# Moving the last output tiles of an attention kernel to the end of their periods, and summing them in another buffer

## The chip, the cores and the metric

The kernel runs on one core of a Trainium2 chip. A core has five engines with queues of their own: TensorE (PE) for matrix products, VectorE (DVE), ScalarE (ACT), GpSimd (POOL), and SyncE (SP), which in this kernel issues every DMA. Each engine works through its queue strictly in the order in which the program wrote it, and waits where an operand isn't ready. PE writes into PSUM, a memory of its own; the other data lie in SBUF. The metric is the device time in microseconds (us).

## The reference, cut to what matters

Two layers work on x of shape (2, 2048, 512): two batches of 2048 rows with 512 features. The first is a state space layer with a feed-forward part and is not touched by the change. The second is self-attention with 16 heads of 32 features, whose norm is modulated by a condition:

```python
h = _sln(hidden, w, ...)                       # layer norm, times gamma, plus beta
qkv = (h @ Wqkv.T + bqkv).reshape(B, N, num_heads, hd, 3)
energy = jnp.einsum('bhqd,bhkd->bhqk', q, k)
att = jax.nn.softmax(energy, axis=-1) / D ** 0.5
out = jnp.einsum('bhqk,bhkd->bhqd', att, v)
out = out @ Wp.T + bp
h1 = out + hidden
h2 = _sln(h1, w, ...)
return h2 + h1
```

The change concerns the last four lines: the projection, the sum with `hidden`, and the second norm with the sum `h2 + h1`. With the row mean m and the reciprocal deviation s, one row of the output is (h1 - m) * s * gamma + beta + h1. The constants of the norm are folded into two rows that are the same for all rows of a batch, `g_row` and `t_row`.

## The kernel before, in words

The attention runs in blocks. A block is one batch, one pair of heads and one chunk of 512 queries; there are 2 x 8 x 4 = 64 blocks. A block has 16 tiles of keys (128 keys each) and takes eight periods of two key tiles. The order of all work is written by hand: one loop over periods `j` (from -22 to 513) issues the instructions, and since every engine works in order, the place in this loop is the place in each engine's queue.

In one period, the loop issues, in this order:

- what is due at its start (a list filled by `after(j, ...)`),
- `make`: scores of one key tile on PE, from which DVE takes off the maximum (L805),
- `compare`: scores that DVE only uses for a running maximum of a later block (L771),
- `exponentials` of the first key tile on ACT (L810),
- `keep`: scores of a later block, copied to SBUF by ACT (L762) and put into the running maximum by DVE (L767),
- `exponentials` of the second key tile,
- what is due at its end (a list filled by `closing(j, ...)`),
- `take_off`: POOL takes the maximum off kept scores that the next period uses (L799, 2.39 us each, 704 of them),
- `weighted`: PE multiplies the probabilities of the period before with the values (L820).

Scores are kept and compared 14 periods ahead. So from period 498 on, PE has no scores to make ahead. PSUM has three slots called `s` for scores; the projections of output tiles take one of them too. Kept scores lie in a ring of 22 buffers, `ring`.

When a block is done, its result and its row sums go to DRAM. When all head pairs of a chunk are done, the chunk's output tiles of 128 rows can be finished. Each batch has 16 such tiles, `qt` 0 to 15. Those of the first batch (b = 0) are finished while the second batch's attention runs. Those of the second batch (b = `LB` = 1) come at the very end. The last two head pairs of the second batch are ordered so that chunks 0, 1 and 2 are done by periods 480, 488 and 496. Their tiles, `qt` 0 to 11, run beside the remaining attention, one every two periods; the change concerns these twelve. The last chunk's four tiles (`qt` 12 to 15) are done together after the last block by `end_last`.

A tile `qt` of the second batch passes through these functions. The first column is the period relative to its start k, where k = 484 + 2 qt:

| period | function | what it issues |
|---|---|---|
| k | `fetch` | SP: loads `o4` (the attention's result), `by` (reciprocal row sums, four DMAs) and `xr` (x plus the bias) |
| k + 2 | `divide` | POOL: `o4` times `by` (L878) |
| k + 3 | `project` | PE: four products into `py` in PSUM (L891) |
| k + 3 | `residual` | DVE: `xr` = `py` + `xr` (L898), which is h1 |
| k + 3 | `statistics` | DVE: mean and variance, first guess of the reciprocal root |
| k + 4 | `deviation` | DVE: three turns of Newton's method on one column, and `shift` |
| k + 5 | `last_norm` | ACT: `z` = normed h1, into PSUM (L958); DVE: `y` = `z` times `g_row` (L960) |
| k + 6 | `last_close` | POOL: h1 + `t_row` (L965), then `y` plus that (L966); SP: stores `y` (L967) |

All of these are issued with `after`, at the start of the period. `y` has one buffer; `xr` has three.

The tiles of the first batch take another way through `turns` (Newton on POOL), `gain` (DVE: `w` = (h1 - m) * `g_row`, and `xr` = h1 + `t_row`, L933 and L934), `scaled` (ACT: `w` times s, L939) and `close` (POOL: one sum, L944; SP: store). Their projections and DVE work are issued with `closing`, at the end of a period. h1 stays in PSUM there.

Near the end, `end_sums`, `end_weights`, `end_sums_more` and `end_x` load what the last chunk needs, also through SP. `end_begin` and `end_project` do part of its projection on PE in periods 510 and 511.

Of the kernel before, what the change touches and what calls it, by code (L numbers as in the profile page):

```python
# [14 lines left out]
ALU = mybir.AluOpType  # L15
# [4 lines left out]
P = 128  # L20
# [19 lines left out]
def tile_s5_block_then_sln_attention(  # L40
# [21 lines left out]
    nc = tc.nc  # L62
# [3 lines left out]
    TT = CH // P  # L66
# [5 lines left out]
    NQ = L // CH  # L72
# [29 lines left out]
    x2 = [dpool.tile([L, D], F32, name=f"x2_{b}") for b in range(NB)]  # L102
# [457 lines left out]
    spare = ps1.tile([P, TT, D], F32, name="spare", tag="po", bufs=1)  # L560
# [47 lines left out]
    for name, src in (("wk", w_kT), ("wq", w_qT), ("wv", w_vT)):  # L608
        w = wlate.tile([P, KC, D], F32, name=name)
# [229 lines left out]
    held, ending = {}, {}  # L839
# [21 lines left out]
    def fetch(b, qt):  # L861

        at = slice(qt * P, (qt + 1) * P)
        o4 = work.tile([P, NG, P], F32, name="o4")
        nc.sync.dma_start(o4, od[b][:, at].rearrange("(g r) q -> r g q", r=P))
        by = work.tile([P, NG, P], F32, name="by")
        heads = invd[b][:, at].rearrange("(g j) q -> j g q", j=4)
        for j in range(4):
            nc.sync.dma_start(
                by[32 * j : 32 * j + 32, :, :], heads[j : j + 1, :, :].to_broadcast([32, NG, P])  # L870
            )
        xr = work.tile([P, D], F32, name="xr", bufs=3)
        nc.sync.dma_start(xr, x2[b][at, :])
        held[b, qt] = o4, by, xr

    def divide(b, qt):
        o4, by, xr = held[b, qt]
# [16 lines left out]
    def residual(b, qt):  # L894

        o4, xr, py = held[b, qt]
        if b == LB:
            nc.vector.tensor_add(xr, py, xr)  # L898
            held[b, qt] = xr, xr, None
        else:  # L900
            nc.vector.tensor_add(py, py, xr)
            held[b, qt] = py, xr, o4.rearrange("p g q -> p (g q)")

    def statistics(b, qt):

# [14 lines left out]
    def newton(eng, y, v):  # L920

        for _ in range(3):
            c = small.tile([P, 1], F32, name="c3")
            eng.tensor_scalar(c, y, y, v, ALU.mult, ALU.mult)
            eng.tensor_scalar(y, c, 1.5, y, ALU.add, ALU.mult)

    def turns(b, qt):
        newton(nc.gpsimd, *held[b, qt][-2:])

    def gain(b, qt):  # L930

# [31 lines left out]
    def last_close(b, qt):  # L963
        h, y = held.pop((b, qt))
        nc.gpsimd.tensor_tensor(h, h, ending[b][1], ALU.add)  # L965
        nc.gpsimd.tensor_tensor(y, y, h, ALU.add)  # L966
        nc.sync.dma_start(out[b, qt * P : (qt + 1) * P, :], y)  # L967

    LB, LC = NB - 1, NQ - 1

    def spare(name):
        return ring.tile([P, 2, CH], F32, name=name, tag="x")
# [121 lines left out]
    for i in range(NP):  # L1097
        w = 2 if i in twice else 1
# [16 lines left out]
    def after(j, what, *args):  # L1115

        due.setdefault(j, []).append((what, args))

    def closing(j, what, *args):

        due.setdefault(j + 0.5, []).append((what, args))
# [13 lines left out]
    for b in range(NB):  # L1135
        for c in range(NQ):
            j = NP * (blocks.index((b, NPAIR - 1, c)) + 1) + 1
            if (b, c) == (LB, LC):
                most, rest = slice(0, NH - 4), slice(NH - 4, NH - 2)
                j = NP * (N - 1)  # L1140
                after(j - 5, fetch_sums, b, c, most)
                after(j - 3, invert, b, c, most)
                for g in range(NG - 1):
                    after(j - 2 + g, end_sums, g)
                after(j + 1, end_weights)
                after(j + 1, end_sums_more)
                after(j + 2, end_x)
                after(j + 1, fetch_sums, b, c, rest, 32)
                after(j + 4, invert, b, c, rest, 32)
                after(j + 5, end_divisors, NG - 1, 2, 1)  # L1150
                for g in range(NG - 1):
                    after(j + 3 + g, end_divide, g)
                for e in (1, 2):
                    after(j + 8, end_divide, NG - 1, slice(HD * e, HD * e + HD))
                after(j + 6, end_begin, 0)
                for g in range(NG - 1):
                    after(j + 6 + g // 2, end_project, 0, [g])
                continue
            after(j, fetch_sums, b, c)
            after(j + 2, invert, b, c)  # L1160
            if c == 0:
                after(j + 2, last_rows, b) if b == LB else after(NP * (NPAIR * NQ * (b + 1) + 2), last_rows, b)
            for t in range(TT):
                qt = c * TT + t
                if b == LB:
                    k = j + 3 + 2 * t
                    after(k, fetch, b, qt)
                    after(k + 2, divide, b, qt)
                    after(k + 3, project, b, qt)
                    after(k + 3, residual, b, qt)  # L1170
                    after(k + 3, statistics, b, qt)
                    after(k + 4, deviation, b, qt)
                    after(k + 5, last_norm, b, qt)
                    after(k + 6, last_close, b, qt)
                else:

                    k = NP * (NPAIR * NQ * (b + 1) + 2 + 3 * qt // 2)
                    after(k, fetch, b, qt)
                    after(k + 3, divide, b, qt)
                    for g in range(NG):  # L1180
                        closing(k + 5 + g // 2, project, b, qt, (g,))
                    closing(k + 7, residual, b, qt)
                    closing(k + 8, statistics, b, qt)
                    closing(k + 9, gain, b, qt)
                    after(k + 11, turns, b, qt)
                    closing(k + 12, scaled, b, qt)
                    after(k + 14, close, b, qt)
# [5 lines left out]
    def block_at(j):  # L1193
        n, i = divmod(j, NP)
        return (n, i) if 0 <= n < N else (None, i)

    for j in range(FIRST, NP * N + 2):
# [20 lines left out]
        now, k = block_at(j)  # L1218
# [89 lines left out]
```

## Time and profile before

| | |
|---|---|
| median of three runs | 3430.34 us (3430.2 to 3431.68) |
| profiled execution | 3433.31 us, its span 3431.5 us |
| mean granted TensorE clock | 0.991 |
| busy: PE, DVE, ACT, POOL | 97%, 62%, 57%, 62% of the span |
| `take_off` L799 | 704 x 2392 ns on POOL |
| projection L891 | 8 records, some 3.5 to 3.7 us a tile, from 3267.5 for tile 0 to 3387.7 for tile 11 |
| L965 and L966 on POOL | 12 each, median 1277 and 1280 ns |
| last result of the attention read from PSUM (L1043) | 3407.4 us |

The span is the time from the first to the last instruction in the profile. A stretch of the trace is named by its start and end in microseconds from the start of the span. A matrix product in 32-bit floats stands as two records in the trace. A group of instructions is named by its line in the kernel: L799 is line 799. In a table of waits, "A <- B" says that A's engine stood still until B was done. "DMA by<-invd" is the transfer that loads `by` from the DRAM tensor `invd`; "SPq" is the queue of SP.

### The profile page before, as it was taken

The page shows a single profiled execution, that of the slowest core. Times are in us where ns is not written, and L with a number is a line of the kernel's source. Part 1 is how long each engine was busy: PE and PEld are TensorE (multiplying, and loading weights), DVE is VectorE, ACT ScalarE, POOL GpSimd, SP SyncE. Part 2 cuts the span into 40 slices and gives each one's busy share as a digit, 9 for nine tenths or more (in the row PEclk, how much of TensorE's full clock was granted, in tenths as well). Part 3 has the DMA queues.
Part 4 walks back from the last instruction along what each step waited for, and adds up shares of the span by engine and source line. Part 5 has one row for each costly group of instructions (what it writes and reads, how often), then busy time and mean ns, then how long its engine had stood idle before and what let it go on. Part 6 is the DMA issues. An engine that isn't in the chain of part 4 may idle for free.

```text
span 3431.5 us, 33641 instructions
## 1 busy us (share of the span) xinstructions
PE 3333.8 (97%) x11380; PEld 1450.9 (42%) x11380; DVE 2129.4 (62%) x2720; ACT 1950.2 (57%) x2208; POOL 2140.0 (62%) x1162
## 2 busy tenths in 40 slices
PE   7999999999999999999999999999999999999997
PEld 4444444444444444433444444444444444444432
DVE  6232323232323220588888888888888888888885
ACT  2111111111111111289999999999888888888863
POOL 4133232313232310189999999998999999999986
PEclk8999999999999999999999999999999999999999
DMA  8001111111111102333132323222334333233233
GB/s 307 1 25 43 46 43 41 43 43 43 44 43 37 43 31 68 104 71 85 48 73 67 73 53 74 70 71 58 78 91 90 72 81 92 69 88 79 61 101 113
DMA packets 201394, 237.02 MB, mean 69 GB/s; under 512 B 89544, under 2 KB 118728, under 8 KB 197126
## 3 DMA queue, kind: packets, MB, share of 16 engines
q1 hardware_dynamic: 201222, 234.87, 25.0%
q8 instruction: 90, 1.47, 0.2%
q14 instruction: 82, 0.67, 0.1%
HBM read 166.77 MB, written 67.76 MB: 68 GB/s over the span
## 4 chain that ended last, share of the span: by engine, by line
PE 61%; DVE 16%; ACT 16%; issue 3%; DMA 2%; POOL 2%; SPq 0%; DVEq 0%; ACTq 0%; POOLq 0%
PE ph L487 13%; PE po L500 13%; PE o L820 9%; DVE run L767 8%; PE s L751 7%; ACT x L762 7%; PE pk L530 6%; ACT x L810 4%; ACT pT L810 4%; PE pv L542 3%; DVE pT L805 3%; PE py L891 2%; DVE run L771 2%; PE pu L421 2%; POOL x L799 1%
## 5 line engine op out<-in xcount | busy, mean ns | idle before, releaser
L799 POOL TENSOR_TENSOR x<-x,shift 128x1024 f32<-128x1024 f32 x704 | 1655.6, 2392 | 138.9 <-DMA shift<-flat 122.8
L751 PE MATMUL s<-qs,ks 128*128 128x512 f32 x2688 | 823.2, 427 | 41.3 <-DVE run L767 28.4
L762 ACT COPY x<-s 128x1024 f32<-128x1024 f32 x704 | 691.7, 1010 | 143.1 <-PE s L751 137.5
L767 DVE TENSOR_TENSOR run<-s,run 128x1024 f32<-128x1024 f32 x576 | 705.1, 1224 | 79.4 <-ACT x L762 35.9
L810 ACT ACTIVATE x<-x 128x1024 f32<-128x1024 f32 x704 | 739.0, 1059 | 20.1 <-POOL x L799 19.6
L820 PE MATMUL o<-x,v 128*64 128x512 f32 x2816 | 717.7, 611 | 1.1 <-ACT x L810 1.1
L751 PEld LDWEIGHTS s<-qs,ks 128*128 128x128 f32 x2688 | 444.2, 189 | 455.1 <-DVE run L767 159.2
L487 PE MATMUL ph<-fT,w_sb 128*128 128x512 f32 x1024 | 463.6, 597 | 0.0
L500 PE MATMUL po<-w_sb,hid 128*128 128x512 f32 x1024 | 460.3, 592 | 0.0
L491 ACT ACTIVATE hid<-ph,vec 128x512 f32<-128x512 f32 x128 | 87.9, 687 | 596.0 <-PE ph L487 596.0
L805 DVE TENSOR_TENSOR pT<-s,shift 128x1024 f32<-128x1024 f32 x320 | 388.8, 1215 | 53.6 <-PE s L751 53.6
L771 DVE TENSOR_TENSOR run<-s,run 128x1024 f32<-128x1024 f32 x320 | 389.1, 1216 | 12.5 <-PE s L751 12.1
L810 ACT ACTIVATE pT<-pT 128x1024 f32<-128x1024 f32 x320 | 339.5, 1061 | 73.9 <-DVE pT L805 73.6
L158 DVE SCALAR_TENSOR_TENSOR lo<-pk,vec,hi 128x512 fp32r<-128x512 f32 x64 | 48.0, 751 | 493.9 <-ACT hi L157 493.9
L820 PE MATMUL o<-pT,v 128*64 128x512 f32 x1280 | 330.2, 594 | 8.9 <-ACT pT L810 8.9
L434 POOL TENSOR_TENSOR m<-m,m 128x512 f32<-128x512 f32 x8 | 13.2, 1644 | 449.8 <-DVE m L432 449.8
L487 PEld LDWEIGHTS ph<-fT,w_sb 128*128 128x128 f32 x1024 | 193.3, 192 | 229.0 <-issue 229.0
L820 PEld LDWEIGHTS o<-x,v 128*64 128x64 f32 x2816 | 157.1, 135 | 311.7 <-issue 237.9
L500 PEld LDWEIGHTS po<-w_sb,hid 128*128 128x128 f32 x1024 | 190.7, 190 | 221.5 <-issue 221.5
L157 ACT ACTIVATE hi<-pk,vec 128x512 fp32r<-128x512 f32 x64 | 44.0, 687 | 383.1 <-PE pk L530 383.1
L510 POOL TENSOR_TENSOR x<-x,gated 128x512 f32<-128x512 f32 x32 | 39.6, 1269 | 354.3 <-DVE gated L509 354.3
L820 PEld LDWEIGHTS o<-pT,v 128*64 128x64 f32 x1280 | 91.4, 137 | 193.8 <-issue 142.2
(250 smaller groups left out, 2494.2 us busy)
## 6 DMA issues: line engine op xcount, KB each, us to landing
ks<-kd SPq DMA_DIRECT2D x128, 256.0 KB
qs<-qd SPq DMA_DIRECT2D x512, 64.0 KB
shift<-flat SPq DMA_DIRECT2D x64, 512.0 KB
x<-in_x SPq DMA_DIRECT2D x8, 1024.0 KB
w_sb<-in_w SPq DMA_DIRECT2D x8, 1024.0 KB
x<-x SPq DMA_DIRECT2D x8, 1024.0 KB
kd<-hi SPq DMA_DIRECT2D x32, 256.0 KB
kd<-lo SPq DMA_DIRECT2D x32, 256.0 KB
```

The lines of the kernel that those rows point to most:

```text
L487: nc.tensor.matmul(ph, w1_sb[:, k, f * P : (f + 1) * P], fts[b, c][:, k, :], start=k == 0, stop=k == KC - 1)
L500: nc.tensor.matmul(pos[b, c][:, t, :], hid[:, t * P : (t + 1) * P], w2_sb[:, f, :], start=f == 0, stop=f == FC - 1,)
L530: nc.tensor.matmul(pk, w[:, k, g * P : (g + 1) * P], hT[:, k, :], start=k == 0, stop=k == KC - 1)
L542: nc.tensor.matmul(pv, fts[b, c][:, k, t * P : (t + 1) * P], wv[:, k, :], start=k == 0, stop=k == KC - 1)
L751: nc.tensor.matmul(s[:, e, :], kst[pair_of[n], e][:, kt * P : (kt + 1) * P], qst[n][:, e, :], start=True, stop=True,)
L762: nc.scalar.copy(x, s)
L767: nc.vector.tensor_tensor(runs[n], s, kept[n, 0] if kt == 1 else runs[n], ALU.max)
L771: nc.vector.tensor_tensor(runs[n], raw_scores(n, kt), runs[n], ALU.max)
L799: nc.gpsimd.tensor_tensor(x, x, shifts[n], ALU.add)
L805: nc.vector.tensor_tensor(x, s, shifts[n], ALU.add)
L810: nc.scalar.activation(x, x, AF.Exp)
L820: nc.tensor.matmul(outs[n][64 * e : 64 * e + 64, :], v[:, kt, e : e + 2, :], x[:, e, :], start=first, stop=final,)
```

## The change

It touches only the twelve tiles of the second batch.

- `xr` is no longer loaded in `fetch` (period k) but by a new function `fetch_x` in period k + 2. For the first batch, `fetch` calls it at once.
- `project`, `residual`, `statistics`, `deviation` and `last_norm` move from the start of their periods to the end of the same periods (`closing` in place of `after`).
- `last_close` writes its final sum into the tile of `xr` (h1), not into `y`, and the store reads it from there.
- Tiles 8 to 11 (`qt >= LAST`) take the way of the first batch: h1 stays in PSUM, Newton's turns run on DVE (`turns` with `nc.vector`), then `gain`, `scaled` and `close`. Their `w` is a buffer of the ring.

```diff
         held[b, qt] = o4, by
+        if b != LB:
+            fetch_x(b, qt)
+
+    def fetch_x(b, qt):
         xr = work.tile([P, D], F32, name="xr", bufs=3)
-        nc.sync.dma_start(xr, x2[b][at, :])
-        held[b, qt] = o4, by, xr
+        nc.sync.dma_start(xr, x2[b][qt * P : (qt + 1) * P, :])
+        held[b, qt] += (xr,)
...
-        if b == LB:
+        if b == LB and qt < LAST:
             nc.vector.tensor_add(xr, py, xr)
             held[b, qt] = xr, xr, None
-        else:
-            nc.vector.tensor_add(py, py, xr)
-            held[b, qt] = py, xr, o4.rearrange("p g q -> p (g q)")
+            return
+        nc.vector.tensor_add(py, py, xr)
+        w = spare("w1")[:, 0, :] if b == LB else o4.rearrange("p g q -> p (g q)")
+        held[b, qt] = py, xr, w
...
-    def turns(b, qt):
-        newton(nc.gpsimd, *held[b, qt][-2:])
+    def turns(b, qt, eng=nc.gpsimd):
+        newton(eng, *held[b, qt][-2:])
...
         nc.gpsimd.tensor_tensor(h, h, ending[b][1], ALU.add)
-        nc.gpsimd.tensor_tensor(y, y, h, ALU.add)
-        nc.sync.dma_start(out[b, qt * P : (qt + 1) * P, :], y)
+        nc.gpsimd.tensor_tensor(h, h, y, ALU.add)
+        nc.sync.dma_start(out[b, qt * P : (qt + 1) * P, :], h)
...
+    LAST = (NQ - 2) * TT
...
                     after(k, fetch, b, qt)
+                    after(k + 2, fetch_x, b, qt)
                     after(k + 2, divide, b, qt)
-                    after(k + 3, project, b, qt)
-                    after(k + 3, residual, b, qt)
-                    after(k + 3, statistics, b, qt)
-                    after(k + 4, deviation, b, qt)
-                    after(k + 5, last_norm, b, qt)
-                    after(k + 6, last_close, b, qt)
+                    closing(k + 3, project, b, qt)
+                    closing(k + 3, residual, b, qt)
+                    closing(k + 3, statistics, b, qt)
+                    if qt < LAST:
+                        closing(k + 4, deviation, b, qt)
+                        closing(k + 5, last_norm, b, qt)
+                        after(k + 6, last_close, b, qt)
+                    else:
+                        closing(k + 4, turns, b, qt, nc.vector)
+                        closing(k + 4, gain, b, qt)
+                        closing(k + 5, scaled, b, qt)
+                        after(k + 6, close, b, qt)
```

More of the change, by code (lines that the diff above doesn't have):

```diff
@@ L871, in fetch @@
             )
+        held[b, qt] = o4, by
+        if b != LB:
+            fetch_x(b, qt)
+    def fetch_x(b, qt):
         xr = work.tile([P, D], F32, name="xr", bufs=3)
-        nc.sync.dma_start(xr, x2[b][at, :])
-        held[b, qt] = o4, by, xr
+        nc.sync.dma_start(xr, x2[b][qt * P : (qt + 1) * P, :])
+        held[b, qt] += (xr,)
     def divide(b, qt):
```

## The prediction

> **What bounds the kernel now.** I first read the page's busy shares: TensorE (PE) 97%, VectorE (DVE) 62%, GpSimd (POOL) 62%. They are averages over four stages. The change works only from 3250 us on, so the next view is the busy time by stretch there: the full periods with tiles 0 to 4 (3267 to 3326), those that run out of scores to make ahead (3326 to 3365), the last block, and the end.
>
> ```profile
> core 0: us, PE busy (x) PEld busy (x) DVE busy (x) ACT busy (x) POOL busy (x), PEclk, DMA share, GB/s
> 3267.00:3326.00 59.00, 54.33 (x185) 21.54 (x181) 50.27 (x97) 36.84 (x41) 52.34 (x29) 1.00 0.39 107
> 3326.00:3365.00 39.00, 34.97 (x120) 13.06 (x121) 29.59 (x69) 20.65 (x24) 36.63 (x22) 1.00 0.47 132
> 3365.00:3407.00 42.00, 36.48 (x114) 13.16 (x112) 19.60 (x49) 17.77 (x20) 37.82 (x27) 0.96 0.38 119
> 3407.00:3431.50 24.50, 11.73 (x30) 5.24 (x28) 16.49 (x28) 0.65 (x2) 3.69 (x14) 0.81 0.12 43
> ```
>
> No engine owns this part. In the first stretch PE is busy 92%, POOL 89%, DVE 85%; afterwards POOL leads with 94% and 90%. So I asked for the waits of POOL and DVE there, and for those of SP's queue, which issues every DMA.
>
> ```profile
> POOL xr L965 <- ACT z L958: 4.2, 4, 2.6
> POOL o L878 <- DMA by<-invd: 0.6, 1, 0.6
> DVE y L960 <- DMA out<-y: 13.9, 3, 5.3
> DVE xr L898 <- PE py L891: 5.4, 10, 1.2
> SPq L967 <- POOL y L966: 35.3, 8, 7.6
> ```
>
> The columns are total us, times, longest. DVE loses 13.9 us because `y` has one buffer, which the store of the tile before still reads. SP stands 35.3 us in front of stores whose sum POOL has not finished; the next tile's loads are queued behind them. The chain of waits shows which of these carries the end:
>
> ```profile
> 3361.10 1.28 POOL y L966
> ...
> 3362.40 0.34 SPq L967
> ...
> 3371.23 5.16 DMA od<-raw
> ...
> 3376.46 0.51 SPq L1009
> ...
> 3380.55 5.57 DMA by<-invd
> ...
> 3386.37 1.28 POOL o L878
> ...
> 3387.69 3.70 PE py L891 x8
> ```
>
> It runs from the closing sums of tile 7 on POOL through SP's queue (store of tile 7, loads of tile 10, the loads for the end, the divisors `by` of tile 11) to the division of tile 11 on POOL. From its projection at 3387.69 PE runs without a pause to its last weighted sum, about 3407.3, and then comes the fixed end of 24 us. **So the division of tile 11 sets the end**, and two things arrive there together: POOL's own row of work, with 0.59 us of idle time just before, and the divisors.
>
> **What the Trainium skill says.** "GPSIMD Engine Reference", 3.1, prices a two-input sum there at about twice VectorE's. The trace agrees: 1.27 us on POOL against 0.69 on DVE for 128x512. "PSUM — Partial Sum Buffer", The four PSUM rules, says that GpSimd cannot touch PSUM; hence `w` and `xr` lie in SBUF. "SBUF — State Buffer", Who interferes with whom, says that a DVE instruction with two SBUF inputs contends with GpSimd. The added ones read one operand from PSUM, so I charge nothing; the first batch runs the same pair (L933, L934) in 0.742 and 0.680 us.
>
> **The change, part by part.**
>
> 1. *One sum less on POOL, tiles 8 to 11.* L965 and L966 (1.27 us each) become one L944 (1.28). Tiles 8 and 9 close before the division of tile 11: 2 x 1.27 = 2.54 us leave the row that sets the end. Tile 10's 1.27 lies behind it, tile 11's behind the last subtraction.
>
> 2. *DVE and ACT for those tiles.* Out: `y` (0.69) and `shift` (0.21). In: L933 and L934, spaced like their twins at the end (0.66 and 0.60). That is +0.36 us a tile in stretches where DVE is busy 76% and 47%; nothing on the path. The waits on the store go (13.9 us), but they were not what POOL waited for: it was idle 0.59 us from 3355.6 to 3399.6. What is late next is the divisors.
>
> 3. *PSUM.* `py` stays in one of three `s` slots for one period more. Score tiles there are at most one a period, so two slots suffice until period 511, where PE has 3.8 us of other work before it wants the slot and DVE needs 1.1 + 1.5 + 1.3 = 3.9: 0.1 us.
>
> 4. *From the start to the end of the period (tiles 0 to 11).* PE makes its scores before the projection (3.5 us), so DVE no longer does residual and statistics (2.1 us and a wait of 0.6) before the `make` addition. At the last projection 0.47 us of scores are already done: a gain of 0.5. Against it, `z` moves behind both exponentials of its period, while the closing sums stay at the start of the next. The trace says that `z` was just in time: POOL waited for it in four of the closes 0 to 6. From the trace I put close 4 together again: DVE's maxima of period 496 end 1.75 us earlier without the deviation ahead of them (3326.8), then deviation (to 3328.55), `make` addition (1.14), exponential (1.0), `z` (0.75): 3331.4. I take 1.4 as given back by earlier periods, where DVE no longer waits 0.6 for each projection while additions are ready (0 to 7.8 by the rivals below). Close 4 begins at 3330.0 instead of 3328.02: **2.0 us lost**.
>
> 5. *`xr` fetched two periods later.* No DMA more or less. The store now reads `xr`, so a fetch waits for the store three tiles before, issued two periods (10 us) earlier; the chain shows 5 to 7.3 us for a landing, so nothing is paid. On SP each fetch of `xr` now stands ahead of the next tile's `o4` and `by`: 0.43 us later. On DVE the residual waits for `xr`; the projection needs division and 3.5 us, about as long as the load. I take nothing; bound 0 to 1 us a tile.
>
> 6. *`w` from the ring.* Four more buffers, freed blocks earlier: nothing.
>
> Sum: from close 4 to the division of tile 11 took 3386.37 - 3328.02 = 58.35 us, of which 0.20 + 0.78 + 0.46 + 0.59 = 2.03 waiting. Without these waits and without 2.54: 53.8. The division begins at 3330.0 + 53.8 = 3383.8, 2.6 earlier; with the 0.5 of part 4 the gain is 3.0. The profiled execution took 3433.31 us (span 3431.5), so 3430.3; against the median 3430.34, **3427.3**.
>
> **Rivals.**
>
> *The divisors decide.* Close 7 ended at 3362.38 and `by` of tile 11 landed at 3386.12: 23.7 us of SP and DMA. Close 7 would now end at 3330.0 + 32.9 = 3362.9; with 0.43 more the divisors are there at 3387.1, 0.9 later than POOL got them. Less the 0.5 of part 4: 3430.7. For it: `by` was late already. Against: fewer stalls make the loads ahead of it start sooner.
>
> *DVE loses nearly all its waits.* From 3268.45 to the `make` addition of period 497, DVE has 26 additions and maxima of 1.14, five times residual and statistics (2.1) and deviation (1.75), four `y` (0.69), two reductions (0.6) and a reciprocal (0.46): 53.4 us. Without a pause this ends at 3321.9, `z` at 3323.6, close 4 4.4 us earlier than now, and 4.4 + 2.03 + 2.54 + 0.47 = 9.4 are won if the divisors keep up; with half a microsecond lost on each of three tiles 7.9: 3422.4. For it: DVE waits in nearly every tile. Against: PE, POOL and DVE are all loaded near 90%, and each wait removed meets another engine.
>
> *Slower: `z` stops POOL.* POOL used to run nearly one period ahead of ACT. The `z` of tile 1 stood at 3291.95 and would stand behind the second exponential, which ended at 3298.5: 6.6 us. If no later period recovers this, and two projections behind three scores wait 1.5 to 2.3 us for a PSUM slot, close 4 is 10.4 late, close 7 ends 10.4 - 1.4 = 9.0 later, the divisors follow, and the end is 9.0 + 0.4 - 0.5 = 8.9 later: 3439.2. For it: POOL has 90% to do and no way to catch up. Against: ACT is busy only 62%, and the `make` additions come earlier. It decides by over 0.2% from a close 7 that ends after 3369.
>
> That the change does not do what it says is not likely: every tile below 8 and above has its own branch.
>
> **How the numbers follow.** A difference under 0.2% (6.9 us) is about what a measurement of this kernel can tell from no change. The forecast has 0.29 and the divisors 0.18; both lie within: 0.47. DVE freed: 0.33, above my sum, since several stalls in a row are easily underrated by hand. `z` stops POOL: 0.20. The range runs from 3420, the 9.4 and a microsecond for shorter gaps, to 3437, most of the slower case; its likeliest part alone is 3425 to 3432.
>
> **What would show it.** `y` waiting on `out` gone; `close`'s sum on POOL 20 times in place of 16; POOL's wait for `z` in closes 1 to 4 longer than 4.2 us in sum; the division of tile 11 near 3383.8 and, if it is later, a wait for `by` before it. Wrong would be: a close 4 that starts before 3327, or a PE that pauses after the projection of tile 11.

## The result, and the profile after

The changed kernel takes **3439.06 us** (median of 12 runs, 3434.17 to 3443.34) against 3431.46 us (12 runs, 3429.71 to 3434.95) for the kernel before in the same session: a ratio of 1.0021, interval 1.0012 to 1.0030. It is slower by 7.6 us, about what the prediction called the smallest difference that can be told here. The forecast of 3427.3 is missed by 11.8 us, and the time lies 2 us above the range.

The profiled execution took 3441.38 us (span 3439.6), 2.3 more than the median. The busy time by stretch, in the form of the prediction's first view, with the later boundaries moved to the same events (`PEclk` is the clock granted to TensorE):

```profile
core 0: us, PE busy (x) PEld busy (x) DVE busy (x) ACT busy (x) POOL busy (x), PEclk, DMA share, GB/s
3267.00:3326.00 59.00, 52.21 (x171) 21.28 (x169) 45.17 (x86) 31.87 (x36) 42.37 (x26) 0.91 0.30 78
3326.00:3368.00 42.00, 38.35 (x123) 14.29 (x121) 29.93 (x71) 21.89 (x25) 38.18 (x22) 0.92 0.45 132
3368.00:3415.50 47.50, 38.12 (x113) 13.88 (x114) 22.39 (x55) 16.96 (x20) 34.18 (x23) 0.93 0.36 116
3415.50:3439.60 24.10, 11.27 (x28) 5.08 (x28) 16.50 (x28) 0.60 (x2) 5.86 (x16) 0.80 0.15 54
```

In the first stretch POOL falls from 89% busy to 72%, DVE from 85% to 77%, and PE's clock from 1.00 to 0.91. The second and third stretches have become 3.0 and 5.5 us longer; the end is what it was. The first looks equally long only because this execution entered it 3.3 us earlier (the copy of block 59's result at 3237.77 instead of 3241.03): 3.4 us are lost there too. The waits of POOL, DVE and PE from 3250 to 3400 (total us, times, longest):

```profile
POOL xr L971 <- ACT z L964: 19.8, 7, 6.8
DVE xr L903 <- PE py L896: 11.2, 4, 3.8
PE py L896 <- POOL o L883: 9.8, 3, 4.9
DVE py L906 <- DMA xr<-x: 9.5, 2, 6.4
PE py L896 <- DVE pT L805: 7.7, 3, 3.0
POOL o L883 <- DMA invd<-sm: 2.1, 1, 2.1
```

`y`'s 13.9 us on its store are gone. In their place POOL waits 19.8 us for `z` (4.2 before), the projection on PE (L896, before L891) waits 9.8 for POOL's division and 7.7 for the `make` addition on DVE (1.1 and 0.4 before), and DVE waits 9.5 for `xr`. The kernel before had one such wait, for tile 0, which the prediction's list of waits leaves out:

```profile
DVE xr L898 <- DMA xr<-x: 2.7, 1, 2.7
```

The part of the chain of waits that answers to the one shown before:

```profile
3367.86 1.27 POOL xr L972
3369.15 0.34 SPq L973
...
3370.51 5.24 DMA by<-invd
...
3382.78 4.48 DMA xr<-x
3387.36 0.71 DVE py L906
...
3390.77 1.10 DMA invd<-sm
3391.95 1.28 POOL o L883
3393.28 6.62 PE py L896 x8
```

Its two ends are the old ones: the closing sums of tile 7, with SP's store behind them, and the division and projection of tile 11. The way between them has to be read with care. The profile puts the last wait of the division down to `invd<-sm`, which stores the divisors of the last chunk, and so leads the chain over DVE and a late `xr`. But the division of tile 11 does not read what that transfer writes. What it needs are the four loads of `by`, and these stand in SP's queue behind the store of tile 7:

```profile
3369.15 0.34 SPq L973 DMA_DIRECT2D out<-xr  x1
...
3383.75 2.13 SPq L869 DMA_DIRECT2D by<-invd  x4
```

That the division waited for these loads is inferred, not shown; before, the same two stood at 3362.40 and 3378.67. What is certainly new is a last projection of 6.62 us instead of 3.70. The list of PE's instructions (start, duration, in brackets the idle time before and its releaser) shows the same in other tiles. Tiles 0, 1, 2, 5, 9 and 10:

```profile
3263.79 3.67 PE L896 MATMUL py<-wp,o 128*128 128x512 f32 x8
3277.24 6.60 PE L896 MATMUL py<-wp,o 128*128 128x512 f32 x8 [2.36 <-DVE pT L805]
3293.73 5.19 PE L896 MATMUL py<-wp,o 128*128 128x512 f32 x8 [3.03 <-DVE pT L805]
...
3331.70 6.67 PE L896 MATMUL py<-wp,o 128*128 128x512 f32 x8 [2.29 <-DVE pT L805]
...
3370.40 3.70 PE L896 MATMUL py<-wp,o 128*128 128x512 f32 x8 [2.79 <-POOL o L883]
3380.47 3.70 PE L896 MATMUL py<-wp,o 128*128 128x512 f32 x8 [2.12 <-POOL o L883]
```

Tiles 1, 2 and 5 belong to the periods in which three score tiles (`make`, `compare`, `keep`) stand ahead of the projection. They fill the three `s` slots, and the first comes free with the `make` addition, which on DVE stands behind `deviation` of the period before. After the pause the same products take 5.2 to 6.7 us: from 3277 to 3284 the granted clock is 0.56. Tiles 9 and 10 paused as long without this.

"TensorE: Matmul & The Clock Gate", Part 1 (The HAM clock gate) of the Trainium skill says that TensorE falls to half its clock after an idle window, and that the window runs freely, so that the effect depends on the phase and varies between runs. The lines agree in this: 6.67 us is 1.8 times 3.67, and of similar pauses some are followed by it and some not. But the page gives a window of about 3.4 us, and these pauses are shorter; the measurement decides.

### The profile page after: what moved, and what is told of

The parts are those of the page before. It is cut to its first block, busy times and chain, and to the rows that moved or that the text cites. A ratio compares the mean times of both kernels' runs of the same rounds, so it can differ in the third digit from the quotient of the medians.

```text
span 3439.6 us, 33644 instructions
## 1 busy us (share of the span) xinstructions
PE 3339.8 (97%) x11380; PEld 1454.2 (42%) x11380; DVE 2130.5 (62%) x2720; ACT 1951.2 (57%) x2208; POOL 2133.7 (62%) x1158
## 4 chain that ended last, share of the span: by engine, by line
PE 62%; ACT 15%; DVE 13%; POOL 4%; issue 3%; DMA 2%; SPq 0%; DVEq 0%; ACTq 0%; POOLq 0%
PE ph L487 13%; PE po L500 13%; PE o L820 10%; PE s L751 8%; DVE run L767 8%; ACT x L762 7%; PE pk L530 6%; ACT x L810 4%; ACT pT L810 4%; POOL x L799 3%; PE pv L542 3%; DVE pT L805 2%; PE py L896 2%; PE pu L421 2%; DVE run L771 1%
```

## The experiments

All are timed against the kernel before in the same session. Since executions already differ by some microseconds where their code is the same, positions are counted from the copy of block 59's result (L829), near 3240 us. The measured values of all runs stand together here; "over before" is the difference of medians, with the ratio's interval. The last three columns are of one profiled execution each: from block 59 to the end of tile 7's closing, from there to the copy of the last result, and what the projections of tiles 0 to 7 took above 3.67 us each. These columns tell where time goes, the medians how much: by the positions the change loses 11.3 us, by the medians 7.6. Where a range is given for the difference of two kernels in "over before", it comes from drawing the recorded executions of both, and of their kernels before, again at random, and holds 95% of the draws.

| kernel | over before, us | ratio's interval | to tile 7 | rest | slow |
|---|---|---|---|---|---|
| before | 0 | | 121.3 | 45.1 | 0 |
| the change | +7.6 | 1.0012 to 1.0030 | 131.4 | 46.3 | 7.5 |
| place_only | +7.2 | 1.0012 to 1.0030 | 128.5 | 46.0 | 3.0 |
| no_place | +0.5 | 0.9995 to 1.0011 | 121.6 | 46.5 | 0 |
| last12 | +7.7 | 1.0012 to 1.0033 | 130.2 | 46.4 | 6.3 |
| warm | +6.8 | 1.0013 to 1.0028 | 127.5 | 45.4 | 0 |
| project_start | +29.1 | 1.0071 to 1.0098 | 149.5 | 48.8 | 3.1 |
| norm_start | +11.2 | 1.0022 to 1.0048 | 135.2 | 46.0 | 7.4 |
| close_late | +7.6 | 1.0015 to 1.0031 | 130.6 | 40.9 | 3.3 |
| deviation_late | +4.9 | 1.0009 to 1.0022 | 126.9 | 44.2 | 1.7 |
| divide_first | +11.7 | 1.0021 to 1.0041 | 129.9 | 45.0 | 3.3 |
| both_first | +5.5 | 1.0010 to 1.0023 | 126.8 | 44.1 | 0 |
| start_divide_first | +12.1 | 1.0022 to 1.0048 | 134.3 | 43.8 | 0.3 |
| no_place_xr | +0.6 | 0.9993 to 1.0009 | 120.4 | 47.1 | 0 |
| project_only | +5.4 | 1.0009 to 1.0024 | 125.1 | 45.4 | 3.1 |
| deviation_start | +4.4 | 1.0007 to 1.0020 | 125.2 | 44.5 | 1.7 |
| warm_two | +4.6 | 1.0006 to 1.0019 | 126.0 | 46.9 | 0 |
| project_only_warm | +1.8 | 0.9997 to 1.0013 | 124.4 | 44.1 | 1.6 |
| deviation_start_warm | +4.6 | 1.0009 to 1.0022 | 125.1 | 45.5 | 1.7 |
| no_place_xr_warm | -0.8 | 0.9990 to 1.0006 | 119.3 | 46.5 | 0 |

One column hardly moves. With the closing sums at k + 6 and the projections at the end, **the rest after tile 7 is 44 to 47 us**, as before. The change's loss lies ahead of tile 7.

### Which part of the change: place_only, no_place, last12

`place_only` is the kernel before with the new places alone; `no_place` is the change with the old places; `last12` lets only one more chunk, 12 tiles, take the old way.

```diff
 place_only (from the kernel before)
-                    after(k + 3, project, b, qt)        # and residual, statistics
-                    after(k + 4, deviation, b, qt)
-                    after(k + 5, last_norm, b, qt)
+                    closing(k + 3, project, b, qt)      # and residual, statistics
+                    closing(k + 4, deviation, b, qt)
+                    closing(k + 5, last_norm, b, qt)
 no_place (from the change): every closing(...) of these tiles becomes after(...)
 last12 (from the change)
-    LAST = (NQ - 2) * TT
+    LAST = (NQ - 1) * TT
```

> Only the place changes: projection to last_norm stand at the end of their periods; xr is fetched as before, y is stored as before, no tile stays in PSUM. Theory slot (a projection behind three score tiles waits until DVE's make addition frees a PSUM slot, PE pauses 2 to 3 us and then runs at half clock): slower than before by 6 to 10 us, with two or three projections of tiles 0 to 7 longer than 5 us. Theory z (POOL stops for z and is late for the rest): slower by 5 to 9 us too, POOL waits for z some 20 us, but projections stay near 3.7 us. Theory late xr (the fetch two periods later stops DVE at the end): within 2 us of before.

> All of the change but the place: what closing issued is issued by after. Theories slot and z: faster than before by 2 to 5 us, since POOL has three sums less before the end and DVE no longer waits on the store (13.9 us before). Theory late xr: slower than before by 3 to 6 us, with waits of DVE on xr near 9 us in tiles 9 and 10.

> The change with LAST = 12, so no tile stays in PSUM: tiles 8 to 11 take two sums on POOL. If the one sum less is a gain that the placement covers up, this is slower than the change by 2 to 4 us. If the PSUM slot that py holds for a period more costs something, it is faster than the change by 2 us or more. If the divisors decide the end, no difference (within 1.5 us).

Measured: +7.2, +0.5 and +7.7 us. The places alone cost all of it that can be told. The other parts together, one sum of POOL less for four tiles, the sum in `xr` and the later `xr`, are worth nothing that can be measured, with or without the new places. `no_place` still shows a wait that could have eaten the gain:

```profile
DVE py L906 <- DMA xr<-x: 10.7, 2, 6.0
POOL xr L971 <- ACT z L964: 4.8, 5, 2.7
POOL o L883 <- DMA by<-invd: 4.5, 2, 3.1
```

### Does the half clock cost anything: warm

Four products on unused data go ahead of the projections of tiles 1, 2 and 5, so that PE does not stand idle.

```diff
+    def warm():
+        pt = ps.tile([P, CH], F32, name="warm", tag="pt")
+        for g in range(NG):
+            nc.tensor.matmul(pt, ident, wp[:, g, :], start=True, stop=True)
+    for j in (489, 491, 497):
+        due[j + 0.5].insert(0, (warm, ()))
```

> The change with four extra products of 128x512 (some 1.85 us of PE) into a PSUM bank of their own, ahead of the projections of tiles 1, 2 and 5, where PE paused 2.4, 3.0 and 2.3 us. They fill pauses and compute nothing that is used. Theory slot with half clock: the three projections fall from 6.6, 5.2 and 6.7 us to 3.7, and the time falls by 4 to 7 us against the change. If the half clock does not matter (z or POOL sets the pace): within 1.5 us of the change or slower.

The three projections fell to 3.60 us each, but the filler took 3.6 us where the pauses were 2.3 to 3.0, and the median stayed at +6.8. Inconclusive: it took away one delay and brought another.

### One place at a time: project_start, norm_start, close_late, deviation_late

```diff
 project_start:  closing(k + 3, project / residual / statistics)  ->  after(k + 3, ...)
 norm_start:     closing(k + 5, last_norm), closing(k + 5, scaled)  ->  after(k + 5, ...)
 close_late:     after(k + 6, last_close)  ->  after(k + 7, last_close)
 deviation_late: closing(k + 4, deviation)  ->  closing(k + 5, deviation)
```

> The change with project, residual and statistics back at the start of their periods; deviation and last_norm (turns, gain, scaled) stay at the end. Theory slot (a projection behind three score tiles waits for a PSUM slot that DVE frees late): near before, within 3 us of it, no PE pause of 2 us in front of the projections of tiles 1, 2 and 5. Theory z (POOL stops for a z that comes behind both exponentials): still slower than before by 5 us or more, with POOL waiting 15 us or more for z.

> The change with last_norm (and scaled) back at the start of their periods; the projection stays behind the scores, at the end. Theory z: near before, within 3 us, POOL waits under 8 us for z. Theory slot: as slow as the change or 1 to 2 us slower, since y (0.69 us) now also stands in front of the make addition that frees the slot; pauses of PE in tiles 1, 2 and 5 of 2.5 to 3.7 us.

> The change with last_close one period later (k + 7), so POOL takes the maximum off one more period of scores before it needs z. Theory z: POOL's waits for z fall from 19.8 us to under 8 and the time by 4 to 8 us. Theory slot: the time stays within 2 us of the change, PE's pauses in tiles 1, 2 and 5 stay at 7.7 us in sum.

> The change with deviation (1.75 us of DVE) moved from the end of period k + 4 to the end of k + 5, ahead of last_norm, so it no longer stands in front of the make addition that frees the projection's PSUM slot. Theory slot: the pauses of PE in tiles 1, 2 and 5 fall from 7.7 us to about 2.5 us in sum, and the time by 3 to 6 us. Theory z: z comes later still (it waits for the deviation), POOL's waits for z grow by 4 us or more, and the time grows by 2 to 5 us.

`project_start` is 29 us slower than before, which no theory had foreseen. Its waits:

```profile
POOL xr L971 <- ACT z L964: 36.5, 8, 7.1
DVE xr L903 <- PE py L896: 20.4, 7, 5.4
PE py L896 <- POOL o L883: 18.6, 8, 3.5
```

They form a ring. `z` of tile t at the end of period k + 5 holds up its closing on POOL at k + 6; the division of tile t + 2 stands behind that closing; its projection at the start of the next period holds up PE with the scores behind it, and so the next `z`.

`norm_start` (+11.2 us) has the longest pauses for a slot, 3.90, 4.64 and 3.90 us, and projections of 6.42, 5.99 and 6.01 us after them. Its POOL waits 22.0 us for `z`, no less than in the change, so the earlier place did not bring `z` earlier, and the run does not tell what an earlier `z` would be worth.

`close_late` takes POOL's wait for `z` down from 19.8 to 5.9 us and gains nothing: POOL waits 10.8 us for divisors instead. Its shorter rest in the table, 40.9, only says that tile 7 now closes a period later.

`deviation_late` takes away the pauses for the slot:

```profile
3277.98 3.67 PE L896 MATMUL py<-wp,o 128*128 128x512 f32 x8 [0.49 <-DVE pT L805]
3289.74 3.67 PE L896 MATMUL py<-wp,o 128*128 128x512 f32 x8 [1.24 <-DVE pT L805]
...
3327.50 5.37 PE L896 MATMUL py<-wp,o 128*128 128x512 f32 x8 [0.49 <-DVE pT L805]
```

Tiles 1 and 2 are back at 3.67 us, and the loss falls to 4.9 us.

### The order on POOL: divide_first, both_first, start_divide_first

The fetch of `xr` and the division of tile t + 2 go ahead of the closing of tile t in the same slot; `both_first` adds this to `deviation_late`, `start_divide_first` to `project_start`.

```diff
-                    after(k + 2, fetch_x, b, qt)
-                    after(k + 2, divide, b, qt)
+                    due.setdefault(k + 2, []).insert(0, (divide, (b, qt)))
+                    due[k + 2].insert(0, (fetch_x, (b, qt)))
```

> The change, with one order altered: the fetch of x's rows (fetch_x) and the division of tile t+2 are issued ahead of the close of tile t in the same slot, not behind it. Measured for the change: 3439.06, PE waits 9.8 us for POOL's division, POOL 19.8 us for z in closes, DVE 9.5 us for xr. Theory A (the projections of the late tiles are late because the division stands behind a close that waits for z): PE's waits on o fall below 4 us, DVE's on xr below 5, POOL's on z stay or grow; the time falls 2 to 4 us, to about 3436. Theory B (only PE's pauses for a PSUM slot behind deviation and the slow clock after them count; the division is late whatever stands ahead of it): within 1 us of the change.

> As divide_first, and with deviation one period later, as in deviation_late (3436.41). If the PSUM pauses (2.7 us) and the division behind the close (theory A) are two separate terms, they add: 3432 to 3434, within 0.1% of the kernel before. If the second is only what the first turns into (theory B), it stays at about 3436.

> As project_start (projections at the start of a period, normalisation at the end; 3460.67), with fetch_x and the division of tile t+2 issued ahead of the close of tile t. If project_start's 29 us come from the ring z, close, division, projection ahead of the scores, next z, the ring is opened here: PE's waits on o fall from 18.6 to below 6 us and the time to 3440 or less. If they come from the projections at the start with the slot held long, it stays above 3452.

In the change the new order gains nothing (+11.7, which is 4.1 above the change, range -1.5 to 7.1), and beside `deviation_late` it does nothing (+5.5). PE's waits for the division stayed at 10.0 us in both, so the closing ahead of it is not all of why it is late: the division then waits for the divisors (7.9 and 6.8 us), and the closing behind it. In `project_start`, the same edit takes 29.1 down to 12.1:

```profile
POOL xr L971 <- ACT z L964: 18.1, 7, 5.7
DVE xr L903 <- PE py L896: 10.4, 4, 5.2
PE py L896 <- POOL o L883: 2.5, 2, 1.3
```

PE's wait for POOL's division fell from 18.6 to 2.5 us, so the ring was some 17 of the 29. The time stayed 3.7 us above the limit set for it; the rest of that kernel is not explained.

### x's rows early: no_place_xr

```diff
 no_place_xr (from no_place)
-                    after(k + 2, fetch_x, b, qt)
+                    after(k + 1, fetch_x, b, qt)
```

> As no_place (only LAST and the sum into h; everything at the start of its period; 3432.88, equal to before), with fetch_x one period earlier, which there cost DVE 10.7 us of waits for xr in tiles 10 and 11. If that wait is what ate the gain of the sum left out (2.5 us for tiles 8 and 9), the time comes out 2 to 4 us below before, 3428 to 3430. If POOL's sum was covered there anyway, within 0.8 us of before.

DVE's wait for `xr` is gone, and the time is that of before (+0.6). The wait was real and lay beside the path, and the sum that POOL saves was covered: the division of tile 11 waited 3.17 us in this profile.

### Projection, deviation and normalisation apart: project_only, deviation_start, warm_two

```diff
 project_only (from the change)
-                        closing(k + 4, deviation, b, qt)   # turns, gain
-                        closing(k + 5, last_norm, b, qt)   # scaled
+                        after(k + 4, deviation, b, qt)
+                        after(k + 5, last_norm, b, qt)
 deviation_start: the first of the two pairs only
 warm_two (from warm)
-        for g in range(NG):
+        for g in range(2):
```

> The change, with only the projection, the residual and the statistics at the end of their period; deviation and the normalisation (for tiles 8 to 11 the turns, the gain and the scaling) are at the start of theirs as before. Theory A (PE's pauses behind deviation, and z half a period late, are the whole price): both are gone, PE's waits on make's addition fall from 7.7 below 1.5 us, and the time is within 1.5 us of the kernel before. Theory B (the place of the projection itself costs, since PE then comes to the next scores late): 3435 or more with neither of the waits.

> As project_only, but the normalisation (last_norm, for tiles 8 to 11 the scaling) at the end of its period, as in the change. Theory A: PE's pauses behind deviation stay away, z is late: POOL waits 10 us or more for z, and the time is 3 to 5 us above project_only's, about 3436, as deviation_late (3436.41). Theory C (z's place costs nothing, only the PSUM pauses and the slow clock after them do): within 1 us of project_only.

> As warm (products on data that is not used, issued ahead of the projections of tiles 1, 2 and 5), with 2 products instead of 4: about 1.8 us by warm's 3.6 us for four, which fits into the pauses of 2.3 to 3.0 us. If the half clock after the pauses is a price of its own (projections of 6.60, 5.19 and 6.67 us instead of 3.67), they fall to about 3.7, and the time falls 3 to 7 us below the change's 3439. If the engines wait elsewhere anyway, the projections fall and the time stays within 1 us of the change's.

With the projection at the end of its period, the four cases are:

| over before, us | normalisation at the start | at the end |
|---|---|---|
| deviation at the start | +5.4 | +4.4 |
| deviation at the end | +11.2 | +7.6 |

The normalisation costs nothing that can be told at the end of its period when the deviation stands at the start (a difference of 1.0 us, range -0.4 to 2.6). The deviation at the end costs 3.2 us (0.7 to 5.5) or 5.8 (3.4 to 11.6, with only five executions of `norm_start`). The projection alone costs about 5 over `no_place` (2.9 to 7.4).

Two things limit this table. It holds with the projection at the end: with the projection at the start, the other two at the end cost 29 us (`project_start`), so the three places are not three prices that can be added in any order. And `project_only` did not lose the pauses for a slot, as had been expected: PE waits 5.0 us for the `make` addition there, ahead of which `y` of another tile now stands at the start of the period. In `deviation_start` these waits are 0.49, 1.24 and 0.49 us, and it still costs 4.4.

`warm_two` keeps the change's places and fills its pauses:

```profile
3279.94 1.88 PE L1207 MATMUL warm<-wp,ident 128*128 128x512 f32 x4
3282.45 3.67 PE L896 MATMUL py<-wp,o 128*128 128x512 f32 x8 [0.63 <-DVE pT L805]
3294.39 1.98 PE L1207 MATMUL warm<-wp,ident 128*128 128x512 f32 x4 [1.40 <-DVE neg L780]
3296.21 3.60 PE L896 MATMUL py<-wp,o 128*128 128x512 f32 x8
```

The projections are at full clock, and the median falls from +7.6 to +4.6, a difference of 3.1 us (range 1.0 to 6.0). The granted clock agrees, and it is known for every execution: its mean is 0.9892 over those of the change and 0.9907 over those of `warm_two`, against 0.9911 for the kernel before in the session of `warm_two`. `warm` shows that the clock alone is not the time: its mean is 0.9904, and it lies at +6.8.

Kernels side by side say the same. The change, `place_only` and `last12`, which have its places for projection and deviation and were neither filled nor reordered, lie at 1.0021 to 1.0023. Those that lose the long pauses of tiles 1, 2 and 5 or the clock after them (`deviation_late`, `both_first`, `deviation_start`, `warm_two`) lie at 1.0013 to 1.0016, on average 2.6 us lower (range 1.3 to 3.9). The groups were made after the results were known. And the single profile does not say how slow a kernel is: `place_only` has 3.0 us of slow projections, the change 7.5, at the same time.

### What is left when the clock is kept: the last three

```diff
+    def warm(products): ...
+    for tile, products in ((1, 2), (2, 2), (11, 4)):      # project_only_warm
+        todo = due[487 + 2 * tile + 0.5]
+        todo.insert(todo.index((project, (LB, tile))), (warm, (products,)))
 deviation_start_warm: ((8, 2), (11, 3)) in deviation_start
 no_place_xr_warm: ((11, 3),) in no_place_xr, at due[487 + 2 * tile]
```

> project_only with products on unused data ahead of the projections of tiles 1 and 2 (two each, about 1.9 us) and 11 (four, 3.6 us), inside pauses that were 2.8 and 5.1 us there. The projections of these tiles ran 5.37, 5.06 and 5.43 us instead of 3.67: 4.9 us at a lower clock. If the lower clock is the price of project_only (3437.31, 5.4 above before), the time falls to 3432 to 3434. If it is the place of the projection itself (z later, POOL waits), it stays above 3435.5.

> deviation_start with such products ahead of the projections of tile 8 (two) and tile 11 (three), where pauses of 2.83 and 3.80 us were followed by 6.58 and 5.40 us. Nothing waits for tile 8's projection soon, as the last sum of tile 7 sets the end: only tile 11's 1.7 us count, so 3434 to 3435.5. If tile 8's clock counts as well, 3432 to 3433.

> no_place_xr (3432.28, before 3431.6) with three such products ahead of the projection of tile 11, which there waited 3.38 us and then took 5.87 us instead of 3.70. The projection falls to 3.7 and all behind it is PE's own work, so the time is 1.5 to 2.2 us lower, 3430 to 3431: just under the kernel before. If PE waits later for ACT or DVE instead, nothing.

`project_only_warm` comes to +1.8 us, no longer to be told from before. It lies 3.6 us under `project_only` (range 1.6 to 6.7), and the mean granted clock of its executions is 0.9908 instead of 0.9897. The projections of tiles 1 and 2 before and with the filler:

```profile
3279.44 5.37 PE L896 MATMUL py<-wp,o 128*128 128x512 f32 x8 [1.09 <-DVE pT L805]
3294.50 5.06 PE L896 MATMUL py<-wp,o 128*128 128x512 f32 x8 [2.84 <-DVE pT L805]
```

```profile
3275.28 3.60 PE L896 MATMUL py<-wp,o 128*128 128x512 f32 x8
3287.03 1.96 PE L1207 MATMUL warm<-wp,ident 128*128 128x512 f32 x4 [1.30 <-DVE y L966]
3288.82 3.60 PE L896 MATMUL py<-wp,o 128*128 128x512 f32 x8
```

Its profiled execution is its fastest run, so the sum of the table's positions should not be leaned on; the medians can be.

`deviation_start_warm` gained nothing (+4.6 after +4.4), but it is a poor test. One filler went ahead of the wrong tile: the pause of 2.83 us and the projection of 6.58 us after it, at 3365.58, are tile 9's, while tile 8's projection, at 3354.80, had waited 0.22 us and run at full clock. And the filler takes a `pt` slot of PSUM; ahead of tile 8 it waited for one that `z` held:

```profile
3361.33 3.57 PE L1207 MATMUL warm<-wp,ident 128*128 128x512 f32 x4 [6.66 <-DVE y L966]
3364.74 3.60 PE L896 MATMUL py<-wp,o 128*128 128x512 f32 x8
```

So tile 8's projection began 10 us later than without the filler. POOL then waited 3.33 us for `w` of tile 8 (not at all without the filler), and with the closing of tile 8 its store came late in SP's queue, and the loads behind it: the division of tile 11 began 24.9 us after the end of close 7 instead of 22.3. Tile 11's filler did its part. Its projection fell from 5.40 to 3.70 us, and from its start to the last copy the time fell by the same 1.7 us (20.96 to 19.26). So in these profiles what one filler won the other lost.

`no_place_xr_warm` has the filler of tile 11 alone. The projection fell from 5.87 to 3.70 us, and from its start to the last copy the time fell by 2.2 us (21.90 to 19.73). In the profile, POOL stands 4.65 us before the division of that tile instead of 3.17, and the division begins 1.6 us later after close 7, which takes most of that away; why is not known. The medians go from +0.6 to -0.8, near what was expected, but both intervals include no difference from the kernel before.

## Why the prediction was wrong

**The frame held.** The end was forecast from a chain that runs from tile 7's closing over SP and the divisors to the division of tile 11. The change fits it, with the way between inferred as said above, and so do nearly all variants by the column "rest". The slower rival took the same frame and named a close 7 after 3369 as the point from which it decides; close 7 ended at 3369.12, and the rival's time of 3439.2 is 0.1 us from the median. The forecast weighed this case at 0.20. Counted from block 59, the profile loses 8.6 us up to the start of close 4, 0.2 from there to the division of tile 11, and 2.9 in tile 11's projection; behind it 0.5 is won, the one gain of step 4 that came as forecast.

**Step 4 failed: 2.0 us for the start of close 4.** Counted from block 59, close 4 starts at 95.6 us instead of 87.0: 8.6 lost. The step moved only `z` and credited 1.4 us to DVE. It forgot what PE does at the new place: behind three score tiles the projection needs the slot that the `make` addition frees, and `deviation`, now at the end of the period before, stands ahead of that addition. (The step did see `deviation` ahead of the addition, but only as a delay for `z`.) The sum of pauses was 7.7 us in tiles 1, 2 and 5. The slower rival had named two of them with 1.5 to 2.3 us each (measured: three, 2.36, 3.03 and 2.29), but the forecast's sum did not use them. With the deviation out of the way (`deviation_late`) the three pauses fell to 0.49, 1.24 and 0.49 us and the loss to 4.9.

**Step 3 asked the wrong tiles.** "Two slots suffice" looked at tiles 8 to 11, where at most one score tile a period is made. The slots ran out in tiles 1, 2 and 5, because the projection came behind the scores, not because `py` was held longer.

**A term was missing altogether: PE's clock.** Projections were taken at 3.5 to 3.7 us wherever they stood. Three of them took 5.19 to 6.67 us ahead of tile 7, 7.5 us in sum above 3.67 each, and tile 11's 6.62. Filling the pauses gave back about 3 us in the change and 3.6 in `project_only`. The profile before had the sign. The table ahead of the prediction gives 3.5 to 3.7 us for all projections, but tile 10's took 4.42, shortly after a pause of 3.08:

```profile
3374.66 1.98 PE L820 MATMUL o<-pT,v 128*64 128x512 f32 x4 [3.08 <-ACT pT L810]
3376.56 4.42 PE L891 MATMUL py<-wp,o 128*128 128x512 f32 x8
```

**Step 1's 2.54 us were not there.** Between close 7 and the division of tile 11 the time fell by 1.2 us only (24.0 to 22.8), and POOL, early with two sums less, stood 2.14 us before the division, by the reading above for its divisors. This is the rival "the divisors decide". `no_place` shows the same at the median: nothing gained. From close 4 to the division the forecast had 53.8 us; the measured 58.6 is that of before (58.35).

**Step 2 was right**: `y`'s waits went, and nothing followed. **Step 5's "nothing" held at the median but not as a wait**: 0 to 1 us a tile was the bound, and tiles 9 and 10 waited 3.13 and 6.37; `no_place_xr` removed such waits without any gain, and `place_only`, with the early fetch, is as slow as the change. Step 6 was nothing, too, in as far as `no_place` holds all of it.

**The slower rival's reason was only in part the right one.** It laid most to `z` behind the second exponential. POOL's waits for `z` did grow, 4.2 to 19.8 us, but the place of `z` did not make them: with `z` at the start (`project_only`) POOL waits 12.7 us for it, with `z` at the end (`deviation_start`) 13.5, and the times can't be told apart. With the closing a period later they fell to 5.9 us and nothing was gained. That the rival's number was nearly exact, with a wrong main term, is luck.

**What stays open.** Going from `no_place` to the change by way of `project_only` and `deviation_start`, the place of the projection costs about 5 us and that of the deviation about 3; by another way the shares would differ, as `project_start` shows. How the former divides between the pauses for a slot, the clock and a delay of its own is not settled: `project_only_warm` leaves 1.8 us, but `warm_two`, with no slow projection ahead of tile 7 in its profile, leaves 4.6, with PE waiting 10.4 us for POOL's divisions of the last tiles. The order on POOL and the later closing were tried for that and are not it.

## What to carry to other kernels

Moving a matrix product behind others in an in-order queue moves it behind their PSUM slots too: list, for every period it will stand in, how many slots are taken ahead of it and what stands before the instruction that frees the next. Price a new pause of the tensor engine with the pause and with the slower clock that may follow. And where a chain through an in-order DMA queue sets the end, ask first whether work saved on an engine beside it can reach that end: here POOL was 90% busy, and sums taken from it brought nothing.

## What the runs showed of the hardware

- In the change, pauses of 2.1 to 3.0 us were followed by projections of 5.2 to 6.7 us instead of 3.67 in three places and by unchanged ones in two. In `deviation_late` one of 5.37 us followed a pause of only 0.49, and in tile 5 the same pause of 1.08 us was followed by 3.67 us in `project_only` and by 5.26 in `project_only_warm`. So the pause just before a product does not tell its clock. With two filler products of 0.9 us each ahead of them, the projections of tiles 1 and 2 took 3.60 to 3.67 us in both kernels that had these.
- Full clock in tile 11's projection shortened the way from its start to the last copy by just what the projection had lost, 1.7 and 2.2 us in two pairs of profiles. At the median neither gain can be told: the division ahead of it came 2.7 and 1.6 us later.
- Profiles of kernels whose code is the same up to there reach the copy of block 59 between 3233.3 and 3241.4 us; positions had to be counted from that event.
